# Four-layer recurrent network on one core: angle passes inside the first attention, third gating inside the last attention's set-up, one bias on GpSimd and one decay on VectorE

## The chip, the cores and the metric

The kernel runs on one core of one Trainium2 chip, as one program with one launch. The metric is device time in microseconds. The engines are named as the profile names them: PE (TensorE matmuls; PEld its weight loads), DVE (VectorE), ACT (ScalarE), POOL (GpSimd), SP (SyncE, which issues most DMAs).

## The reference

Four layers, each of two parts. `x` has 4096 tokens (8 x 512, or the same tokens in other groupings) of 128 features; everything is float32. Each layer is

```python
xn = layernorm(x)
s = attention(xn)          # L0 sliding window, L1 recurrence, L2 local + latent, L3 see below
g = silu(ffn(xn))          # L0 low-rank quantised, L1 experts, L2 see below, L3 soft slots
x = x + s * g              # "gating"
```

What the change touches is in the third feed-forward and the last attention:

```python
# L2 ffn
real = x @ cos(theta + theta_noise);  imag = x @ sin(phi + phi_noise)
return sqrt(real * real + imag * imag)

# L3 attention: 16 heads of 64 complex features
ang = t[:, None, None] * om                       # t: position, om: frequencies
qr, kr = q * (cos(ang) + i sin(ang)), k * (cos(ang) + i sin(ang))
E = exp(clip(-mu * |t - t'|, -30, 0))             # per head: "decay"
V = sigma2 / (2 mu) * (1 - E * E) + eta2 + gamma2 # per head: "variance"
maha = max(|q|^2 + E * E * |k|^2 - 2 E * Re(qr . conj(kr)), 0) / V
logits = coef * log1p(maha / nu) - 32 * log(V)
logits = where(t >= t', logits, -inf)             # causal
out = softmax(logits) @ v @ Wo
```

`coef * log1p(maha / nu)` is computed as `coef * log(maha * V + nu * V)` with `coef * log V` taken into a second table, so a head has three tables over the causal half of the positions (128 x 1280): `E`, `V` (nu times the variance) and `G` (log of the variance times a factor of the head, and -1e30 where the key is later than the query: "bias").

## The kernel before

The activations lie transposed in SBUF (features on the partitions, tokens along the row): `x`, `xn` and `s`, 128 x 4096 each, are there for the whole program. `network` runs the parts one after the other: `layer_norm`, attention, feed-forward with its gating (`gated_add`), four times. A planner places the instructions: each goes to its engine by program order and by when its inputs, its tile memory and the engine are expected to be ready, so that an instruction without a mark can move ahead of earlier ones into idle time. An instruction issued through `net.in_order(engine)` is marked: marked instructions of one engine keep their order among themselves. Tile memory is a stack of pools; a tile in memory that an earlier pool held waits until that pool's last reader is done.

*First attention* (`l0_attention`, L203). 64 units `u` of half of the heads for 128 queries. In unit `u` PE turns the weights of `u` (`turned`), ACT copies them (`pt`), PE makes the scores of `u + 3` (`sc`), DVE scales and masks them (`e`) and takes the maximum (`mx`), POOL subtracts it, ACT takes the exponential of `u + 2`, and PE weighs the values (`weigh`, `av`). In every second unit DVE divides the sums (`norm`: `rec`, then `o`) and PE turns them (`tpo`). All of it is marked.

*Angles and sines* (`Prepared.angles`, L1968, and `sines`, L1985). For each of four groups of features DVE multiplies the positions by the frequencies (`ang`, 128 x 512), reduces the angle to one turn (`turn`, L1270: six passes over `ang` and `turns`) and takes the absolute value (`cos`). ACT then makes the cosines, sines and negated sines (128 x 2048 each), and SP stores the three in DRAM (`trig`), from where each head of the last attention loads its own (`ct`, `sn`). Before, all of this lies between the third attention and the last one: `angles` in front of `l2_ffn`, `sines` behind it.

*Third feed-forward* (`l2_ffn`, L1281). 16 matmuls of 128 x 512, squares on ACT, a sum on DVE (`g`), square roots and silu on ACT (marked), and the gating: DVE multiplies (`pr`), POOL adds to `x`.

*Last attention* (`l3_attention`, L1309). The set-up makes the distances `dt` and the causal mask `later` (0 or -1e30, 128 x 1280) on POOL and DVE, the tables of head 0 (`Tables`: `decay`, `exp`, `squares`, `variance`, `variance_nu`, `log`, `bias`), the products `wvo` of the value and output weights (`ps_vo`), and then the norm. The main loop runs over 64 pairs of batches (4 per head) in software-pipelined steps: `STEP` is an order written out by hand, in which `"1 rotate 0"` is part `rotate` of batch 0 of the pair one ahead of the step's, and `"T1 decay"` is part `decay` of the next head's tables, in each fourth step with remainder 1. All of it is marked, so every engine works through `STEP` in this order. The parts that the texts name: `rotate` (DVE, `r<-sn`, `r<-ct`, and a DMA `rs<-r` on SP that swaps halves), `turned` (POOL, `r<-r,rs`), `scores` (PE, `sc<-r`), `key_terms` (POOL, four `ek<-E,kn`), `halved`, `scaled`, `distances` (DVE), `log` (ACT), `logits` (DVE, `y<-y,coef,G`), `maxima` (DVE), `exps` (ACT), `turn`, `weigh`, `values` (PE), `normalise` (ACT), `add` (POOL, `s<-s,o`). ACT's table sets for logarithm and exponential are loaded twice a step.

In the profile, marked instructions all bear line L82 (the helper), so they are told apart by their tiles.

Of the kernel before, what the change touches and what calls it, by code (L numbers as in the profile page):

```python
# [16 lines left out]
P = 128  # L17
B = 8
S = 512
# [183 lines left out]
def l0_attention(net, xn, s_out):  # L203
# [6 lines left out]
    with ExitStack() as st:  # L210
# [152 lines left out]
        for u in range(N + 2):  # L363
# [17 lines left out]
            next(todo, None)  # L381

# [887 lines left out]
def turn(nc, pool, ang, shape, tag):  # L1270

    k = pool.tile(shape, F32, tag=tag, name=tag)
    nc.vector.tensor_scalar(k, ang, 1.0 / (2 * math.pi), ROUND, ALU.mult, ALU.add)
    nc.vector.tensor_scalar(k, k, ROUND, None, ALU.subtract)
    for part in TWO_PI_PARTS:
        nc.vector.scalar_tensor_tensor(ang, k, -part, ang, ALU.mult, ALU.add)
    pi = float.fromhex("0x1.921fb4p+1")
    nc.vector.tensor_scalar(ang, ang, pi, -pi, ALU.min, ALU.max)
# [30 lines left out]
def l3_attention(net, x, xn, s_out):  # L1309
# [9 lines left out]
    with ExitStack() as st:  # L1319
        p1 = st.enter_context(tc.tile_pool(name="a3_1", bufs=1))  # L1320
        pw = st.enter_context(tc.tile_pool(name="a3_w", bufs=2))
        p2 = st.enter_context(tc.tile_pool(name="a3_2", bufs=2))
        p3 = st.enter_context(tc.tile_pool(name="a3_3", bufs=3))
# [7 lines left out]
        later = p1.tile([P, PK], F32, tag="later", name="later")  # L1331
        nc.gpsimd.memset(later, 0.0)
        with tc.tile_pool(name="a3_d", bufs=1) as pd:
            di = pd.tile([P, PK], I32, tag="di", name="di")
            for i in range(NQ):
                cols = slice(off[i], off[i] + w[i])
                nc.gpsimd.iota(di[:, cols], pattern=[[-1, w[i]]], base=P * i, channel_multiplier=1)
                nc.gpsimd.affine_select(
                    out=later[:, cols], in_=later[:, cols], compare_op=ALU.is_ge, fill=NEG,
                    base=P * i, pattern=[[-1, w[i]]], channel_multiplier=1,  # L1340
                )
# [17 lines left out]
        class Tables:  # L1359
# [24 lines left out]
            def decay(self):  # L1384
                pool.tensor_scalar(self.E, dt, nmu[:, self.hs], -30.0, ALU.mult, ALU.max)
# [20 lines left out]
            def bias(self):  # L1406
                G = self.G
                dve.scalar_tensor_tensor(G, G, g_v[:, self.hs], later, ALU.mult, ALU.add)
# [5 lines left out]
        with tc.tile_pool(name="a3_v", bufs=2, space=PSUM) as p_v, tc.tile_pool(  # L1414
            name="a3_vw", bufs=2
        ) as p_vw:
            for g in range(4):
# [9 lines left out]
                nc.scalar.copy(wvo[:, 4 * g : 4 * g + 4, :], ps)  # L1427
            net.layer_norm(x, xn)

        p_s = st.enter_context(tc.tile_pool(name="a3_s", bufs=1, space=PSUM))  # L1430
# [9 lines left out]
        class Pair:  # L1440
# [188 lines left out]
            "0 scores 1", "-1 exps 0 3", "1 key_lengths 0", "-1 exps 0 0", "-1 turn 0 2",  # L1629
            "T1 decay", "0 halved 1", "-1 keep 0 2", "1 key_terms 0", "1 query_norms 0",  # L1630
            "-1 turn 0 0", "-1 exps 1 0", "-2 normalise 1", "1 query_lengths 0", "1 project 1 0",
            "1 turned 0", "0 scaled 1", "-1 exps 1 1", "-1 turn 0 1", "0 distances 1",
            "-1 keep 0 0", "1 project 1 1", "-2 add 0", "-1 keep 0 1", "1 rotate 1", "-1 weigh 0",
            "-1 inverse", "-1 turn 1 2", "0 log", "-1 turn 1 1", "0 logits", "T3 log",
            "1 scores 0", "T3 bias", "0 maxima 2", "-1 keep 1 2", "1 squares 1", "-1 keep 1 1",
            "0 values 0", "1 turned 1", "1 key_norms 1", "-1 normalise 0", "2 project 0 0",
            "0 keep_values 0", "1 halved 0", "1 key_lengths 1", "1 query_norms 1", "0 maxima 1",
            "-1 turn 1 0", "1 query_lengths 1", "T2 variance", "2 project 0 1", "0 exps 0 1",
            "0 values 1", "1 key_terms 1", "-1 keep 1 0", "T2 variance_nu", "-2 add 1", "T1 exp",
            "-1 weigh 1", "1 scaled 0", "2 squares 0", "0 maxima 3", "0 exps 1 2", "T1 squares",  # L1640
            "0 exps 1 3", "1 distances 0", "2 rotate 0", "2 key_norms 0", "0 keep_values 1",
# [498 lines left out]
```

## Time and profile before

| | us |
|---|---|
| median of the 3 runs | 2870.13 |
| lowest, highest | 2869.78, 2882.57 |
| the profiled execution | 2865.32 |
| its span, first to last instruction | 2863.6 |

Where the stages lie in the span (from the timeline, us): first norm and first attention to about 315, first feed-forward to 440, second norm to 466, the second layer to 890, third norm to 923, third attention to 1250, third gating to 1289, norm of the last layer (with the set-up of the last attention around it) to 1329, last attention's pairs to about 2700, last feed-forward to the end.

A line of a group has the engine, operation, tiles (output<-inputs), shape and count, then busy us and mean ns of one, then the idle time before it and who ended it. A line of the timeline has start, duration, engine, operation and tiles. In a busy table each engine's column is busy us with the number of instructions in brackets. A line of the waits has who waited for whom, us in total, times and the longest.

### The profile page before, as it was taken

How to read it: one execution, taken by the hardware profiler on the slowest of the kernel's cores; microseconds unless marked ns; L12 is line 12 of the kernel's file. 1: busy time of each engine (PE TensorE's matmuls, PEld its weight loads, DVE VectorE, ACT ScalarE, POOL GpSimd, SP SyncE). 2: the span in 40 equal slices, each digit the busy share in tenths (PEclk: the TensorE clock that was granted, in tenths of full speed). 3: DMA queues.
4: the chain of work that ended last, by engine and by line, in shares of the span. 5: the costliest groups of instructions: out<-in, count | busy, mean ns of one | idle time of the engine just before them, and what ended most of it. 6: DMA issues, size and time to landing. Idle time of an engine off the chain costs nothing. (4 is left out here: it accounts for less than half of the span.)

```text
span 2863.6 us, 48763 instructions
## 1 busy us (share of the span) xinstructions
PE 2575.9 (90%) x18636; PEld 1801.4 (63%) x18636; DVE 2195.4 (77%) x2907; ACT 1835.7 (64%) x3587; POOL 1556.8 (54%) x1262
## 2 busy tenths in 40 slices
PE   7999898688778889977999999999999999999887
PEld 5666666455335555535677777677777777777674
DVE  4777454566663666664999999999999999999565
ACT  2666342245331455452899888898888889888734
POOL 2444221532342333335677877877877787777323
PEclk7999797899898899877999999999999999999989
DMA  1000002112100000003222222222222222222000
GB/s 48 2 2 2 1 1 89 30 51 46 32 28 17 2 2 2 2 23 92 62 61 57 49 62 61 61 61 57 54 57 61 62 56 66 55 52 52 25 1 30
DMA packets 56310, 112.73 MB, mean 39 GB/s; under 512 B 10768, under 2 KB 28752, under 8 KB 55440
## 3 DMA queue, kind: packets, MB, share of 16 engines
q1 hardware_dynamic: 51584, 99.40, 13.2%
q0 software_dynamic: 4352, 8.92, 1.3%
q8 instruction: 148, 2.42, 0.4%
q10 hardware_dynamic: 144, 1.31, 0.1%
q14 instruction: 82, 0.67, 0.1%
HBM read 30.43 MB, written 12.06 MB: 15 GB/s over the span
## 5 line engine op out<-in xcount | busy, mean ns | idle before, releaser
L82 POOL TENSOR_TENSOR ek<-E,kn 128x512 f32<-128x512 f32 (+3 forms) x512 | 427.1, 867 | 63.2 <-ACT kn L82 62.1
L82 POOL TENSOR_TENSOR r<-r,rs 128x1024 f32<-128x1024 f32 x128 | 317.9, 2484 | 252.9 <-DMA rs<-r 213.1
L82 POOL TENSOR_TENSOR e<-e,mx 128x1024 f32<-128x1024 f32 x112 | 212.6, 1898 | 333.8 <-DVE mx L82 195.5
L82 ACT ACTIVATE y<-y,mx 128x256 f32<-128x256 f32 (+3 forms) x512 | 287.2, 562 | 101.2 <-DVE mx L82 101.1
L82 PE MATMUL sc<-r 128*128 128x512 f32 (+3 forms) x1024 | 307.9, 444 | 24.6 <-POOL r L82 18.8
L82 PEld LDWEIGHTS ps_av<-u,at 128*128 128x128 f32 x2560 | 302.3, 193 | 41.2 <-ACT at L82 31.3
L82 PE MATMUL ps_av<-u,at 128*128 128x128 f32 x2560 | 315.1, 279 | 6.5 <-ACT at L82 6.5
L82 PEld LDWEIGHTS sc<-r 128*128 128x128 f32 x1024 | 166.4, 192 | 176.5 <-issue 71.7
L82 DVE SCALAR_TENSOR_TENSOR y<-sc,qn,V 128x512 f32<-128x512 f32 (+3 forms) x512 | 246.0, 543 | 2.3
L82 ACT ACT_TABLE_LOAD x167 | 214.3, 1283 | 4.1 <-PE pa L82 1.2
L82 DVE TENSOR_REDUCE mx<-y 128x2 f32<-128x768 f32 (+3 forms) x256 | 207.7, 812 | 1.7
L82 DVE SCALAR_TENSOR_TENSOR sc<-sc,ek 128x1280 f32<-128x1280 f32 x128 | 191.3, 1495 | 12.5 <-PE sc L82 6.2
L82 PE MATMUL tp<-ident,y 128*128 128x128 f32 x1280 | 198.5, 278 | 1.2 <-ACT y L82 0.8
L82 DVE SCALAR_TENSOR_TENSOR y<-y,coef,G 128x2560 f32<-128x2560 f32 x64 | 195.7, 3058 | 4.6 <-ACT y L82 2.3
L82 ACT COPY at<-tp 128x512 f32<-128x512 f32 (+1 forms) x384 | 188.2, 512 | 7.8 <-PE tp L82 7.7
L82 DVE TENSOR_TENSOR sc<-sc,E 128x1280 f32<-128x1280 f32 x128 | 191.1, 1493 | 0.0
L82 PEld LDWEIGHTS tp<-ident,y 128*128 128x128 f32 x1280 | 154.3, 146 | 41.4 <-issue 18.3
L82 POOL TENSOR_TENSOR s<-s,o 128x512 f32<-128x512 f32 x120 | 162.6, 1356 | 31.1 <-ACT o L82 31.1
L82 PEld LDWEIGHTS ps_u<-wvo,xn 128*128 128x128 f32 x1024 | 128.3, 191 | 69.2 <-DVE qn L82 55.2
L82 DVE TENSOR_TENSOR r<-sn,ps_kq 128x1024 f32<-128x1024 f32 x128 | 154.9, 1210 | 7.6 <-ACT sq L82 4.1
L82 ACT ACTIVATE y<-y 128x2560 f32<-128x2560 f32 x64 | 149.7, 2339 | 15.6 <-DVE y L82 8.1
L82 PE MATMUL tp<-ident,e 128*128 128x128 f32 x896 | 135.0, 294 | 23.6 <-ACT rt L82 14.4
(396 smaller groups left out, 5779.4 us busy)
## 6 DMA issues: line engine op xcount, KB each, us to landing
rs<-r SPq DMA_DIRECT2D x256, 256.0 KB
yrows<-yy SPq DMA_DIRECT2D x36, 128.0 KB
ct<-trig SPq DMA_DIRECT2D x16, 256.0 KB
m_w<-m_w SPq DMA_DIRECT2D x1, 2560.0 KB
x<-x SPq DMA_DIRECT2D x8, 256.0 KB
xrows<-row SPq DMA_DIRECT2D x8, 256.0 KB
sn<-trig SPq DMA_DIRECT2D x32, 64.0 KB
sn<-trig SPq DMA_DIRECT2D x16, 128.0 KB
```

Of the source, the lines that this page charges most:

```text
L82: ins = op(*args, **kwargs)
```

## The change

- The angle passes become a generator (`turning`, and `angles` with a `yield` after each pass). `network` opens it before the first attention (load of the frequencies and the iota of the positions), and `l0_attention` issues one pass, marked on DVE, at the end of each of the first eight units and of every odd unit after that.
- `angles` now uses the pool of the first layer (`prep_0`), which stays open over the second norm; `sines` (three ACT operations and three DMAs on SP) follows that norm.
- `l2_ffn` is called inside `l3_attention`, after the tables of head 0 and `wvo` and before the norm; the pools `a3_2` and `a3_3` open after that.
- `later` is gone. `bias` multiplies on POOL and sets the causal corner of each query tile with four `affine_select` of 128 x 128 on POOL; `decay` moves from POOL to DVE.
- `STEP` has a new order; `decay` and `exp` of the next head's tables move from remainder 1 to 0.

```diff
--- before.py
+++ after.py
@@ -200,7 +200,7 @@
             )
 
 
-def l0_attention(net, xn, s_out):
+def l0_attention(net, xn, s_out, extra):
 
 
     nc, tc = net.nc, net.tc
@@ -379,6 +379,10 @@
             if u >= U and u % U == 1:
                 finish(u // U - 1)
             next(todo, None)
+            if u % 2 or u < 8:
+                next(extra, None)
+        for _ in extra:
+            pass
 
 
 def l0_ffn(net, x, xn, s):
@@ -1269,13 +1273,23 @@
 
 def turn(nc, pool, ang, shape, tag):
 
+    for _ in turning(nc.vector, pool, ang, shape, tag):
+        pass
+
+
+def turning(dve, pool, ang, shape, tag):
+
     k = pool.tile(shape, F32, tag=tag, name=tag)
-    nc.vector.tensor_scalar(k, ang, 1.0 / (2 * math.pi), ROUND, ALU.mult, ALU.add)
-    nc.vector.tensor_scalar(k, k, ROUND, None, ALU.subtract)
+    dve.tensor_scalar(k, ang, 1.0 / (2 * math.pi), ROUND, ALU.mult, ALU.add)
+    yield
+    dve.tensor_scalar(k, k, ROUND, None, ALU.subtract)
+    yield
     for part in TWO_PI_PARTS:
-        nc.vector.scalar_tensor_tensor(ang, k, -part, ang, ALU.mult, ALU.add)
+        dve.scalar_tensor_tensor(ang, k, -part, ang, ALU.mult, ALU.add)
+        yield
     pi = float.fromhex("0x1.921fb4p+1")
-    nc.vector.tensor_scalar(ang, ang, pi, -pi, ALU.min, ALU.max)
+    dve.tensor_scalar(ang, ang, pi, -pi, ALU.min, ALU.max)
+    yield
 
 
 def l2_ffn(net, x, xn, s):
@@ -1319,8 +1333,6 @@
     with ExitStack() as st:
         p1 = st.enter_context(tc.tile_pool(name="a3_1", bufs=1))
         pw = st.enter_context(tc.tile_pool(name="a3_w", bufs=2))
-        p2 = st.enter_context(tc.tile_pool(name="a3_2", bufs=2))
-        p3 = st.enter_context(tc.tile_pool(name="a3_3", bufs=3))
 
         sp, nmu, v_e2, v_0, coef, k_0, q_0, g_v = net.prep.scalars
         nu = sp[:, 3, :]
@@ -1328,17 +1340,11 @@
         wvo = p1.tile([P, H, P], F32, tag="wvo", name="wvo")
 
         dt = p1.tile([P, PK], F32, tag="dt", name="dt")
-        later = p1.tile([P, PK], F32, tag="later", name="later")
-        nc.gpsimd.memset(later, 0.0)
         with tc.tile_pool(name="a3_d", bufs=1) as pd:
             di = pd.tile([P, PK], I32, tag="di", name="di")
             for i in range(NQ):
                 cols = slice(off[i], off[i] + w[i])
                 nc.gpsimd.iota(di[:, cols], pattern=[[-1, w[i]]], base=P * i, channel_multiplier=1)
-                nc.gpsimd.affine_select(
-                    out=later[:, cols], in_=later[:, cols], compare_op=ALU.is_ge, fill=NEG,
-                    base=P * i, pattern=[[-1, w[i]]], channel_multiplier=1,
-                )
             nc.vector.tensor_copy(dt, di)
         nc.vector.scalar_tensor_tensor(dt, dt, -1.0, dt, ALU.mult, ALU.max)
 
@@ -1382,7 +1388,7 @@
                 )
 
             def decay(self):
-                pool.tensor_scalar(self.E, dt, nmu[:, self.hs], -30.0, ALU.mult, ALU.max)
+                dve.tensor_scalar(self.E, dt, nmu[:, self.hs], -30.0, ALU.mult, ALU.max)
 
             def exp(self):
                 table_set("exp_and_others")
@@ -1404,8 +1410,15 @@
                 act.activation(self.G, self.G, AF.Ln)
 
             def bias(self):
+
                 G = self.G
-                dve.scalar_tensor_tensor(G, G, g_v[:, self.hs], later, ALU.mult, ALU.add)
+                pool.tensor_scalar(G, G, g_v[:, self.hs], 1.0, ALU.mult, ALU.mult)
+                for i in range(NQ):
+                    last = G[:, off[i] + P * i : off[i] + P * i + P]
+                    pool.affine_select(
+                        out=last, in_=last, compare_op=ALU.is_ge, fill=NEG,
+                        base=0, pattern=[[-1, P]], channel_multiplier=1,
+                    )
 
         tables = {}
         T = tables[0] = Tables(0)
@@ -1425,8 +1438,11 @@
                         ps[:, i, :], lhsT=wv[:, i, :], rhs=wo[:, i, :], start=True, stop=True
                     )
                 nc.scalar.copy(wvo[:, 4 * g : 4 * g + 4, :], ps)
+            l2_ffn(net, x, xn, s_out)
             net.layer_norm(x, xn)
 
+        p2 = st.enter_context(tc.tile_pool(name="a3_2", bufs=2))
+        p3 = st.enter_context(tc.tile_pool(name="a3_3", bufs=3))
         p_s = st.enter_context(tc.tile_pool(name="a3_s", bufs=1, space=PSUM))
         p_kq = st.enter_context(tc.tile_pool(name="a3_kq", bufs=1, space=PSUM))
         p_j = st.enter_context(tc.tile_pool(name="a3_j", bufs=2, space=PSUM))
@@ -1626,20 +1642,20 @@
 
 
         STEP = (
-            "0 scores 1", "-1 exps 0 3", "1 key_lengths 0", "-1 exps 0 0", "-1 turn 0 2",
-            "T1 decay", "0 halved 1", "-1 keep 0 2", "1 key_terms 0", "1 query_norms 0",
-            "-1 turn 0 0", "-1 exps 1 0", "-2 normalise 1", "1 query_lengths 0", "1 project 1 0",
-            "1 turned 0", "0 scaled 1", "-1 exps 1 1", "-1 turn 0 1", "0 distances 1",
-            "-1 keep 0 0", "1 project 1 1", "-2 add 0", "-1 keep 0 1", "1 rotate 1", "-1 weigh 0",
-            "-1 inverse", "-1 turn 1 2", "0 log", "-1 turn 1 1", "0 logits", "T3 log",
-            "1 scores 0", "T3 bias", "0 maxima 2", "-1 keep 1 2", "1 squares 1", "-1 keep 1 1",
-            "0 values 0", "1 turned 1", "1 key_norms 1", "-1 normalise 0", "2 project 0 0",
-            "0 keep_values 0", "1 halved 0", "1 key_lengths 1", "1 query_norms 1", "0 maxima 1",
-            "-1 turn 1 0", "1 query_lengths 1", "T2 variance", "2 project 0 1", "0 exps 0 1",
-            "0 values 1", "1 key_terms 1", "-1 keep 1 0", "T2 variance_nu", "-2 add 1", "T1 exp",
-            "-1 weigh 1", "1 scaled 0", "2 squares 0", "0 maxima 3", "0 exps 1 2", "T1 squares",
-            "0 exps 1 3", "1 distances 0", "2 rotate 0", "2 key_norms 0", "0 keep_values 1",
-            "0 exps 0 2", "0 maxima 0",
+            "1 project 0 1", "0 key_terms 1", "-1 maxima 3", "-2 weigh 1", "-1 values 1",
+            "-1 exps 0 1", "1 squares 0", "-1 exps 1 1", "-1 exps 1 2", "1 key_norms 0",
+            "-1 keep_values 1", "-1 exps 0 3", "0 distances 0", "0 scores 1", "-1 exps 1 3",
+            "-1 turn 0 2", "1 key_lengths 0", "-1 exps 0 2", "-1 keep 0 2", "T1 squares",
+            "T0 decay", "-1 turn 0 0", "T2 variance", "1 rotate 0", "-1 maxima 0", "-1 exps 0 0",
+            "1 query_norms 0", "0 halved 1", "-1 keep 0 0", "0 scaled 1", "1 key_terms 0",
+            "-1 exps 1 0", "1 project 1 0", "-2 normalise 1", "1 query_lengths 0", "1 turned 0",
+            "-1 turn 0 1", "-1 keep 0 1", "1 project 1 1", "0 distances 1", "-1 weigh 0",
+            "1 rotate 1", "0 log", "-1 turn 1 2", "-1 turn 1 1", "-1 keep 1 2", "1 squares 1",
+            "T3 log", "1 scores 0", "-1 inverse", "-1 keep 1 1", "-1 normalise 0", "0 logits",
+            "-2 add 1", "0 maxima 1", "1 key_norms 1", "-1 turn 1 0", "1 key_lengths 1", "T3 bias",
+            "1 turned 1", "1 halved 0", "2 project 0 0", "T2 variance_nu", "-1 keep 1 0",
+            "0 maxima 2", "-1 add 0", "0 values 0", "T0 exp", "0 keep_values 0", "1 query_norms 1",
+            "1 scaled 0", "1 query_lengths 1",
         )
         for t in range(-2, N + 3):
             if t + 2 < N:
@@ -1975,12 +1991,17 @@
         ti = pt.tile([P, S], I32, tag="ti", name="ti")
         nc.gpsimd.iota(ti, pattern=[[1, S]], base=0, channel_multiplier=0)
         tt = pt.tile([P, S], F32, tag="tt", name="tt")
-        net.in_order(nc.vector).tensor_copy(tt, ti)
+        yield
+        dve = net.in_order(nc.vector)
+        dve.tensor_copy(tt, ti)
+        yield
         for g in range(4):
             a = self.ang3[:, g, :]
-            nc.vector.tensor_scalar(a, tt, om[:, g : g + 1], None, ALU.mult)
-            turn(nc, pt, a, [P, S], "turns3")
-            nc.vector.scalar_tensor_tensor(self.cos[:, g, :], a, -1.0, a, ALU.mult, ALU.max)
+            dve.tensor_scalar(a, tt, om[:, g : g + 1], None, ALU.mult)
+            yield
+            yield from turning(dve, pt, a, [P, S], "turns3")
+            dve.scalar_tensor_tensor(self.cos[:, g, :], a, -1.0, a, ALU.mult, ALU.max)
+            yield
 
     def sines(self):
 
@@ -2046,19 +2067,20 @@
         prep = net.prep = Prepared(net, ctx)
         with tc.tile_pool(name="prep_0", bufs=1) as p0:
             net.layer_norm(x, xn)
-            l0_attention(net, xn, s)
+            angles = prep.angles(p0)
+            next(angles)
+            l0_attention(net, xn, s, angles)
             prep.l0_decode(p0)
             l0_ffn(net, x, xn, s)
-        net.layer_norm(x, xn)
+            net.layer_norm(x, xn)
+            prep.sines()
         l1_layer(net, x, xn, s)
         net.layer_norm(x, xn)
         with tc.tile_pool(name="prep_t", bufs=1) as pt:
             prep.l2_weights(pt)
             l2_attention(net, xn, s)
-            prep.angles(pt)
             prep.l3_scalars()
-            l2_ffn(net, x, xn, s)
-            prep.sines()
+
         l3_attention(net, x, xn, s)
         l3_ffn(net, x, xn, s, out)
```

## Prediction

> **What bounds the kernel now.** I read the page first: no engine is the bound of the whole, and DVE goes from about half busy to 9 tenths in slices 24 to 37.
>
> ```profile
> PE 2575.9 (90%) x18636; PEld 1801.4 (63%) x18636; DVE 2195.4 (77%) x2907; ACT 1835.7 (64%) x3587; POOL 1556.8 (54%) x1262
> DVE  4777454566663666664999999999999999999565
> ```
>
> Then the busy time by stage (columns: stretch, its length, busy us of PE, PEld, DVE, ACT, POOL, granted clock, DMA share, GB/s), for the four stages that the change touches:
>
> ```profile
> 60.00:120.00 60.00, 57.30 (x684) 36.89 (x682) 38.90 (x44) 36.86 (x58) 26.15 (x15) 0.90 0.01 2
> ...
> 1250.00:1292.00 42.00, 26.05 (x50) 11.50 (x51) 32.25 (x46) 29.41 (x39) 12.87 (x8) 0.70 0.16 66
> 1292.00:1340.00 48.00, 39.10 (x177) 32.37 (x177) 15.78 (x23) 10.56 (x15) 23.77 (x18) 0.69 0.31 91
> ...
> 1440.00:2600.00 1160.00, 1129.43 (x6637) 828.99 (x6636) 1147.62 (x1342) 1035.46 (x2181) 913.21 (x715) 1.00 0.23 58
> ```
>
> The first attention (60:120) is PE's, the last attention's loop (1440:2600) is DVE's: 12 us of 1160 idle. Between them, 1250:1340 (third gating, set-up and norm of the last attention) is bound by no engine: a chain. Third, the loop's groups by shape (busy us, mean ns):
>
> ```profile
> L82 DVE SCALAR_TENSOR_TENSOR y<-y,coef,G 128x2560 f32<-128x2560 f32 x56 | 172.6, 3082 | 2.0
> L82 DVE SCALAR_TENSOR_TENSOR G<-G,g_v,later 128x1280 f32<-128x1280 f32 x13 | 20.1, 1545 | 0.0
> L82 POOL TENSOR_SCALAR E<-dt,nmu 128x1280 f32<-128x1280 f32 x14 | 64.3, 4592 | 1.3
> L82 POOL TENSOR_SCALAR V<-G,sp 128x1280 f32<-128x1280 f32 x14 | 18.7, 1339 | 0.0
> ```
>
> Fourth, POOL's and DVE's timelines around one `y<-y,coef,G` that is longer than the rest (start, duration):
>
> ```profile
> 1538.63 4.59 POOL L82 TENSOR_SCALAR E<-dt,nmu 128x1280 f32<-128x1280 f32 x1
> 1543.29 3.33 POOL L82 TENSOR_TENSOR ek<-E,kn 128x512 f32<-128x512 f32 x4
> 1546.58 2.39 POOL L82 TENSOR_TENSOR r<-r,rs 128x1024 f32<-128x1024 f32 x1
> 1548.91 1.29 POOL L82 TENSOR_TENSOR s<-s,o 128x512 f32<-128x512 f32 x1
> ...
> 1548.88 4.00 DVE L82 SCALAR_TENSOR_TENSOR y<-y,coef,G 128x2560 f32<-128x2560 f32 x1
> ...
> 1193.37 1.50 DVE L82 TENSOR_SCALAR xp<-xp 128x64 f32<-128x64 f32 x1
> ```
>
> To see: the decay (`E<-dt`) makes POOL late by 4.59 us; its `s` add then falls on DVE's logits, which take 4.00 instead of 2.885: the two exclude each other. The last line is a one-input DVE operation that takes 0.20 us elsewhere and 1.50 us against a POOL subtraction.
>
> From start to start of the 64 logits (1361.26 to 2683.13) are 63 steps, 1321.9 us. An undisturbed step is 20.40 us, and 63 of them are 1285.2. The other 36.7 us lie in two steps of each four: 21.74 where the bias `G<-G` runs on DVE (+1.34), about 21.5 where POOL carries the decay.
>
> **Part 1, the last attention's loop (15 heads; head 0 is in the set-up).** Removed from DVE: 15 biases at 1.34 us of pace: -20.1. Removed from POOL: the decay, 4.59 us a head, and with it the late steps: 36.7 - 20.1 = -16.6. POOL takes the bias instead: one multiply like `V<-G,sp` (same operation, 1.34) and four 128x128 selects at the 0.29 of the `later` select, 2.5 us. Its table work falls from 9.65 (4.59 + 2.32 + 1.40 + 1.34) to 7.6 a head, and is spread over more steps.
> Added to DVE: the decay. Nearest row: `ang<-tt,a_om` 128x512, 0.474 us with one scalar from memory; DVE's copy `dt<-di` of 128x1280 takes 0.82. So 0.87, 0.80 of pace: +12.0. It also needs what POOL holds. It stands behind `distances 0`, where POOL is about in its four `ek` (1.27, 1.00, 0.73, 0.46). Bounds: 0 us, and the rest of such a run, 3.3. The `xp` row waited for one instruction; at 1548.88 POOL's next instruction went in ahead. I take 0.6, half of a long `ek`: +9.0. Behind the waiting decay are rotate 0, maxima 0 and halved 1, with ACT's exps waiting for the maxima.
> The written order is new throughout. Per step, start to start, PE needs about 19.6 us (from the back-to-back starts of 1441 to 1461) and ACT 18.3 with both table loads; so it can keep 20.40, but PE has 0.8 to spare. Where ACT takes `T3 log` (1.25) between squares 1 and keep 1 1, PE's values are late by more than that: +0.2 a head, +3.0 (ends 0 and 0.5 a head).
> Sum: -20.1 - 16.6 + 12.0 + 9.0 + 3.0 = **-12.7 us**.
>
> Two rules of the Trainium skill stand against this part. "GPSIMD Engine Reference", Engine selection, sends elementwise work to VectorE but calls GpSimd's one-input operations roughly line-rate. The V row agrees (1.34); the decay row (4.59) doesn't. By the rule the decay costs POOL 1.3 us, its removal wins little, the -16.6 goes, and part 1 is +3.9; by the row, -12.7. The row decides. "SBUF — State Buffer", in its section on the two sides, says that whichever of the two engines starts first keeps the shared ports for the whole instruction; then a waiting decay pays for one POOL instruction (1.27 at most of an `ek`), not for a run. The 1548.88 row leaves the run open.
>
> **Part 2, third gating inside the set-up.** Now the set-up's work for head 0 lies in the norm behind the gating. After the last `x` add this norm takes 39.9 us, where the second norm takes 25.5:
>
> ```profile
> 437.66 2.87 POOL L162 TENSOR_TENSOR x<-x,pr 128x512 f32<-128x512 f32 x2 [4.17 <-DVE pr L161]
> 465.36 0.69 DVE L141 TENSOR_TENSOR xn<-xn,ps 128x512 f32<-128x512 f32 x1 [0.21 <-PE ps L101]
> ...
> 1276.07 12.87 POOL L162 TENSOR_TENSOR x<-x,pr 128x512 f32<-128x512 f32 x8 [28.48 <-DVE pr L161]
> 1328.10 0.69 DVE L141 TENSOR_TENSOR xn<-xn,ps 128x512 f32<-128x512 f32 x1 [1.02 <-PE ps L101]
> ```
>
> In between lie decay 4.6, squares and two scalings 5.1, `later` 3 us on POOL in front of or between the `rstd` powers; the three sines (2.0 + 1.9 + 1.9 and a table load) on ACT in front of the squares; 6.3 us of `ps_vo` matmuls on PE. With these in front: 25.5 - 39.9 = -14.4. They come into the gating's 17 us of matmuls, where POOL idles 28 us. POOL's 6.5 to 7.6 us and DVE's decay are covered there. PE isn't idle: `ps_vo` adds 0 to 6.3 us. ACT's sum there is 9.6 of squares, 2.3 of copies, 2.5 for exp and log, 2.6 for loads: 17.0, as long as the matmuls. I take +4. The loop's first logarithm comes behind the gating's square root and silu now and needs its table again: 1.28 on an ACT that idles 7.25 us in front of it, so 0. The set-up's eight weight loads and table 0's six on SP come before a norm that needs none of them. Sum **-10.4 us** (ends -14 and 0). The angle passes (about 18 us on DVE) leave this stage too, but it isn't DVE's: its `g` adds wait for ACT. I count 0.
>
> **Part 3, the angles in the first attention.** 33 passes: one copy 0.42 and four times 0.47 + 0.42 + 0.42 + 3 x 0.69 + 0.42 + 0.69: 18.4 us of DVE. Cover: in 60:300 DVE waits 50.1 us for PE's scores. Against it: PE waits for DVE's `o` already:
>
> ```profile
> DVE e L82 <- PE sc L82: 50.1, 36, 4.2
> PE tpo L82 <- DVE o L82: 3.5, 14, 0.2
> ```
>
> A pass sits behind a unit's maximum, ahead of the next norm (`rec`, `o`), for which PE's `tpo` waits, and against POOL's subtraction (1.90 us), for which ACT's exp waits. About half of the norms have no slack (14 of 29), and each is pushed by 0.3 to 0.6: 14 x 0.45 = 6; some of it comes back. I take **+5 us** (ends 0 and 18.4, or 25 with POOL's turns). The iota (0.56 on POOL) and the small load move to the start, in front of nothing.
>
> **Part 4, sines behind the second norm.** 5.8 us and a load of 1.28 on ACT, ordered only against marked ACT work, so they can fall into gaps of the first feed-forward or into the norm: 0 to 7, I take 1. Their three 1 MB stores go into SP's queue there, and their memory, with the norm now stacked on it, must be free before the next layer's loads: `m_w` was issued at 440.5 and used at 537 (slack), the router weights are used at 466, at once: 0 to 4, I take 1. **+2 us.**
>
> **Sum**: -12.7 - 10.4 + 5 + 2 = -16.1 us. The profiled execution took 2865.3 (span 2863.6), so 2849; the median of the three runs is 2870.1, 4.8 above it: **2854 us**. A difference under 0.5% (14 us) is about what a measurement here can't tell from none.
>
> **Rivals.**
> - *The decay is held by POOL (slower).* If POOL's queued instructions keep going in ahead, a decay that meets the run of `ek` waits 3.3 us: 15 x (3.3 - 0.6) = +40, 2894. For: 1548.88. Against: the rule, `xp`. From a mean wait of 1.7 us the whole gain is gone, from 2.6 it is slower by over 0.5%. PE with its 0.8 us to spare would show alike: 0.8 us of new waits in 50 steps is 40 us.
> - *The moved work lands on the path.* Passes 18, gating +6 beyond my 4, loads 4: 16.1 of gain less 13 + 6 + 2 more: 2875, within 0.5%. For: PE busy 57 of 60 us in the first attention.
> - *All is covered.* No decay wait, no late log (-12), passes and sines free (-7), `ps_vo` free (-4): 2831.
> - *It doesn't do what it says*: the marks order only marked work, so sines or set-up may stay where they collide; then -10.4 shrinks to about 0: 2864.
>
> **Numbers.** Forecast 0.55 (own range 2836 to 2868), work on the path or not moved 0.19, held decay or PE 0.18, all covered 0.08. Faster: 0.42 of the forecast's 0.55 and the 0.08, 0.50. Slower: the 0.18 and 0.03 of the second: 0.21. Same: 0.29. The range leaves out half of the held case and a little at the bottom: 2832 to 2888.
>
> **What would show it.** Right: logits 2.89 throughout, steps of 20.4 with one of about 21.8 in four; E on DVE 0.9 to 1.5; last `x` add to last `xn` about 26 us; PE's wait for `o` up by some us in the first attention. Wrong: E on DVE over 2.5; undisturbed steps over 20.6 (the order, PE); a norm still near 40; a first attention longer by over 12.

## The result and the profile after

The changed kernel takes 2903.15 us (median of 7 runs, 2893.29 to 2911.06), the kernel before, run beside it, 2868.86 (2863.51 to 2882.57): a ratio of 1.0109, interval 1.0081 to 1.0137. It is slower by 1.1%, where 2854 was forecast. The profiled execution took 2911.06 against 2865.32, a span of 2909.3 against 2863.6: 45.7 us to explain. The medians lie 34.3 apart: the profiled execution of the kernel after is the slowest of its seven, and that of the kernel before is 3.5 under its median.

First the page: the engines' sums, and the rows of DVE and of the granted TensorE clock. The kernel after:

```profile
PE 2618.5 (90%) x18636; PEld 1828.8 (63%) x18636; DVE 2185.2 (75%) x2907; ACT 1845.1 (63%) x3588; POOL 1513.3 (52%) x1321
DVE  4566635446665466663799999999999999999665
PEclk8687768789989889897899999999999999999979
```

and the clock row of the kernel before, which the prediction left out:

```profile
PEclk7999797899898899877999999999999999999989
```

PE has the same 18636 matmuls and is busy 42.6 us longer. In slices 1 to 4 its clock row has 6877 where it was 9997: the first attention. Then the busy table over exactly that attention, from its first projection to its last sum (stretch, length, busy us of PE, PEld, DVE, ACT, POOL, granted clock, DMA share, GB/s), before:

```profile
45.75:321.20 275.45, 257.15 (x3264) 168.29 (x3264) 189.29 (x217) 167.91 (x265) 123.41 (x67) 0.94 0.01 2
```

and after:

```profile
42.51:387.38 344.87, 320.74 (x3264) 206.27 (x3264) 208.19 (x250) 170.54 (x265) 126.28 (x67) 0.74 0.01 1
60.00:120.00 60.00, 55.65 (x502) 35.75 (x500) 35.14 (x42) 25.18 (x40) 19.88 (x10) 0.66 0.00 1
```

The stage is 69.4 us longer. DVE has the 33 passes more (217 to 250 instructions, busy 18.9 us longer). PE's idle time (length less busy) grows from 18.3 to 24.1, by 5.8 us; its busy time grows by 63.6 us for the same 3264 matmuls. So the passes made PE wait hardly longer, but made it run slower: the clock fell from 0.94 to 0.74. "Clock lost" below is the length times what the clock lacks of 1, added up from the trace's clock record: 16.5 us before, 88.8 after, a difference of 72.3.

How one drop begins, from the timeline of after (start, duration, idle time ahead and who ended it):

```profile
196.04 0.74 DVE L82 TENSOR_SCALAR s<-ps_o,a_b 128x512 f32<-128x512 f32 x1
196.70 0.80 DVE L82 TENSOR_SCALAR kb<-ps_k,hm,kbias 128x512 f32<-128x512 f32 x1
197.42 1.32 DVE L82 SCALAR_TENSOR_TENSOR cos<-ang 128x512 f32<-128x512 f32 x1
...
198.66 0.24 DVE L82 RECIPROCAL rec<-av 128x16 f32<-128x16 f32 x1
198.94 0.29 DVE L82 TENSOR_TENSOR o<-av,rec 128x128 f32<-128x128 f32 x1
...
199.38 0.44 PE L82 MATMUL tpo<-ident,o 128*128 128x128 f32 x1 [0.87 <-ACT pt L82]
...
199.75 1.88 PE L82 MATMUL av<-vw,pt 128*64 128x9 f32 x32
...
201.56 2.08 PE L82 MATMUL ps_q<-xn,a_w 128*128 128x512 f32 x2
```

The pass `cos` (1.32 against a POOL subtraction, 0.69 in the kernel before) stands ahead of `rec` and `o`, and `tpo` starts behind a PE gap of 0.87. The profile puts this gap down to ACT's copy `pt`, which ended 0.04 us after `o`; at the same place of before, `tpo` starts at 203.06 without a gap while these copies still run (202.83 to 203.89), so the wait is for `o`. At once `av` takes 1.88 (1.12 at 193.74) and `ps_q` 2.08 (`ps_o`, of the same shape, 1.12 at 194.79): about half speed. The busy table around it:

```profile
189.10:196.00 6.90, 6.54 (x88) 4.31 (x89) 5.39 (x5) 4.12 (x6) 3.07 (x2) 1.00 0.01 2
196.00:199.40 3.40, 2.05 (x17) 0.79 (x15) 3.37 (x7) 1.74 (x3) 1.90 (x1) 1.00 0.01 2
199.40:202.80 3.40, 3.40 (x35) 2.64 (x36) 2.18 (x2) 1.31 (x2) 0.94 (x1) 0.50 0.00 0
```

One stretch of 3.4 us with PE busy 2.05, and the next is at 0.50. How one persists, another stretch of after:

```profile
141.40:165.30 23.90, 23.90 (x166) 14.19 (x165) 12.44 (x16) 9.52 (x15) 7.60 (x4) 0.50 0.01 1
```

PE is busy all of 23.9 us and stays at half. "TensorE: Matmul & The Clock Gate" of the Trainium skill, Part 1 (The HAM clock gate), gives a window of about 3.4 us: half speed after at least one idle window, full speed after one busy one. The window agrees: the lengths in the record (6.8, 13.7, 20.5, 23.9) are multiples of 3.41. The conditions do not: no window ahead of a drop was idle (of the nine drops after 60 us, seven follow gaps of at most 0.9 us, the others of 2.0 and 2.6), and seven busy windows in a row did not bring the clock back. By this rule, if a window is called idle or busy by PE's busy time, this attention would have lost next to no clock; by the record it lost 88.8 us. The measurement decides. The page's section on a second failure mode, micro-idling between groups of matmuls, comes nearer to what is seen.

The waits in 60:300, after:

```profile
DVE e L82 <- PE sc L82: 74.8, 35, 5.2
PE tpo L82 <- DVE o L82: 8.1, 9, 2.6
```

PE's wait for `o` grew from 3.5 to 8.1, and the waits of PE that the view lists in this stretch sum to 13.1 where they were 9.4. That is the size of the prediction's +5 us, and it is all that PE's waits show of a cost of 69.

Last, the loop's groups by shape (1440:2600, busy us, mean ns), and its busy table:

```profile
L82 DVE SCALAR_TENSOR_TENSOR y<-y,coef,G 128x2560 f32<-128x2560 f32 x56 | 161.6, 2885 | 2.2
L82 POOL TENSOR_SCALAR G<-G,g_v 128x1280 f32<-128x1280 f32 x14 | 23.6, 1687 | 46.3 <-ACT G L82 46.3
L82 DVE TENSOR_SCALAR E<-dt,nmu 128x1280 f32<-128x1280 f32 x14 | 19.2, 1375 | 0.0
L82 POOL TENSOR_SCALAR V<-G,sp 128x1280 f32<-128x1280 f32 x14 | 18.7, 1334 | 0.0
L82 POOL TENSOR_SCALAR_AFFINE_SELECT G<-G 128x128 f32<-128x128 f32 x56 | 14.6, 292 | 1.0
```

```profile
1440.00:2600.00 1160.00, 1140.12 (x6726) 839.67 (x6726) 1151.55 (x1360) 1055.34 (x2212) 878.84 (x776) 1.00 0.24 60
```

All logits take 2.885 us now (3.082 before), and the steps are 20.40 with one of 21.56 in four. From the first to the last logits it is 1301.8 us, 20.0 less than before.

The account of the 45.7 us, from stage to stage of the two traces: first attention +69.4; router's matmuls, behind the second norm, +8.8; last attention's loop -20.0; third gating, set-up and norm up to the first logits -3.5 (110.9 to 107.4); first norm -3.2; all else -5.8.

### The profile page after: what moved, and what is told of

Its sections match the earlier page's. It is cut to its first block, busy times and chain, and to the rows that moved or that the text cites. A ratio compares the mean times of both kernels' runs of the same rounds, so it can differ in the third digit from the quotient of the medians.

```text
span 2909.3 us, 49020 instructions
## 1 busy us (share of the span) xinstructions
PE 2618.5 (90%) x18636; PEld 1828.8 (63%) x18636; DVE 2185.2 (75%) x2907; ACT 1845.1 (63%) x3588; POOL 1513.3 (52%) x1321
## 5 line engine op out<-in xcount | busy, mean ns | idle before, releaser
L82 POOL TENSOR_TENSOR ek<-E,kn 128x512 f32<-128x512 f32 (+3 forms) x512 | 435.7, 885 | 48.5 <-ACT kn L82 48.4
L82 POOL TENSOR_TENSOR r<-r,rs 128x1024 f32<-128x1024 f32 x128 | 302.3, 2362 | 237.2 <-DMA rs<-r 215.7
L82 ACT COPY at<-tp 128x512 f32<-128x512 f32 (+1 forms) x384 | 198.4, 517 | 43.2 <-PE tp L82 41.8
L82 DVE TENSOR_REDUCE mx<-y 128x2 f32<-128x512 f32 (+3 forms) x256 | 207.6, 812 | 2.2
L82 PE MATMUL tp<-ident,y 128*128 128x128 f32 x1280 | 183.3, 274 | 9.3 <-ACT at L82 7.5
L82 DVE SCALAR_TENSOR_TENSOR y<-y,coef,G 128x2560 f32<-128x2560 f32 x64 | 184.6, 2885 | 4.9 <-ACT y L82 2.3
L82 PE MATMUL tp<-ident,e 128*128 128x128 f32 x896 | 155.4, 325 | 22.6 <-ACT rt L82 14.4
L82 DVE SCALAR_TENSOR_TENSOR e<-sc,maskFalse 128x1024 f32<-128x1024 f32 (+1 forms) x96 | 90.2, 954 | 108.0 <-PE sc L82 108.0
L82 PEld LDWEIGHTS tp<-ident,e 128*128 128x128 f32 x896 | 125.5, 168 | 64.5 <-issue 34.6
L82 ACT COPY pt<-tp 128x512 f32<-128x512 f32 x224 | 121.8, 584 | 66.5 <-PE tp L82 66.0
```

Of the source, the lines that this page charges most:

```text
L82: ins = op(*args, **kwargs)
```

## The experiments

The theory was the clock: a pass ahead of the norm opens a gap on PE, the clock falls to half and stays there until a batch's dense projections come. The rival was the queue: every pass and its turn with POOL lengthen the chain DVE, POOL, ACT by 2 us (33 x 2 = 66), and a slow PE only follows. Each ratio below is to executions of before made beside that run (their medians are 2856.9 to 2867.1), so times of different runs are compared by their ratios. The table gathers what the profiles show of the first attention, one profile of each kernel.

| kernel | attention, us | clock lost, us | length less clock lost |
|---|---|---|---|
| before | 275.4 | 16.5 | 258.9 |
| after | 344.9 | 88.8 | 256.1 |
| p_after | 276.1 | 16.9 | 259.3 |
| p_even | 299.4 | 42.1 | 257.3 |
| p_fill | 304.4 | 32.7 | 271.6 |
| fill_only | 280.6 | 12.3 | 268.3 |
| b_extra | 331.0 | 69.9 | 261.1 |
| b_late | 317.4 | 52.9 | 264.5 |
| b_early | 293.4 | 32.3 | 261.1 |
| b_late6 | 364.3 | 100.1 | 264.2 |
| b_early6 | 308.5 | 39.9 | 268.6 |

**Is it the passes' place?** `p_after` issues them behind the attention, `b_extra` adds 33 such passes to the kernel before.

```diff
-            l0_attention(net, xn, s, angles)
+            l0_attention(net, xn, s, iter(()))
+            for _ in angles:
+                pass
```

> The changed kernel with its 33 angle passes in one run on VectorE behind the first attention instead of one a unit inside it; all else as changed. Clock theory (the passes hold up the norm, TensorE gets gaps, its granted clock falls to half and stays there until the next batch's projections): half-clock time inside the first attention falls from 178 us to about 33, the attention from 345 to about 275, and 18 us of passes lie in the first feed-forward, partly beside its 30 us of other work: the kernel comes to 2830 to 2850. Queue theory (each pass lengthens the VectorE-GpSimd-ScalarE chain by 2 us, the clock only follows): the same stage time, so this run does not tell the two apart; it says whether the passes' place costs the whole 69 us. If the attention stays over 300, the cause is another part of the change (memory layout, an earlier load).

2839.54 us, a ratio to before of 0.9934 (0.9910 to 0.9957); the attention is back at 276.1. So the whole 69 us came with the passes' place. The executions without a kept trace agree: over the seven of each kernel, the span times the granted clock is 2638 to 2649 us in after and 2634 to 2645 in `p_after`, while the clock lost is 255 and 196 us in the mean.

> The kernel before with 33 further passes of the same shapes in the first attention, one at the end of each odd unit and of the first eight, their results never used; nothing else is changed. Both theories: the attention goes from 275 to about 345 and the kernel from 2869 to about 2938, with half-clock time near 178 us. If it costs under 30 us, the passes alone are not the cause and something else of the change in that stage is.

2911.46 us, 1.0192 (1.0162 to 1.0221); +55.6 us on the attention, of which 53.4 clock. Less than the 70 expected, but most of the cost comes with the passes alone; the changed memory layout and loads are in `p_after` too and cost its attention nothing.

**Queue or clock?** Three kernels keep all 33 passes inside. `p_even` issues them, from the ninth unit on, in front of the scores' `e` instead of the norm:

```diff
-            if u % 2 or u < 8:
+            if u % 2 == 0 or u < 8:
```

> The changed kernel with the same 33 passes, still one a unit inside the first attention, at the end of even units (and of the first eight) instead of odd ones: ahead of the next scores, which VectorE waits for anyway, instead of ahead of the next norm. Clock theory: TensorE's wait for o disappears, the half-clock time falls to 30 to 70 us and the attention to 280 to 300; the kernel comes to 2835 to 2855. Queue theory: the same number of passes in the same chain cost the same, attention about 345, kernel about 2903.

2846.25 us, 0.9960 (0.9950 to 0.9969); attention 299.4. The same DVE work costs 24 us here and 69 there, and both differences are clock (25.6 and 72.3). Up to 115 us, which takes in the first eight units, with a pass each in both kernels, both lose 26 us of clock; behind that `p_even` loses 16 and after 63. `p_fill` gives PE more to do:

```diff
+            pe.matmul(
+                tp[:, 2:4, :], lhsT=net.ident, rhs=w[:, 0:2, :], start=True, stop=True
+            )
             pe.transpose(tp[:, 0, :], o.rearrange("p h d -> p (h d)"), net.ident)
```

> The changed kernel with the passes where the change put them, and one further matmul (identity by 128x256 of weights, its result never read) on TensorE ahead of each of the 32 transposes tpo: it fills the gap in which TensorE waits for o. Clock theory: the gaps are gone or shorter and a dense matmul lies in each, so the clock stays at full speed for most of the attention; although TensorE has 32 x 0.56 = 18 us more to do, the attention falls from 345 to 285 to 310. Queue theory: more work on the busiest engine can only lengthen it: 345 to 363.

2848.64 us, 0.9965 (0.9947 to 0.9983). The busy table over its attention:

```profile
43.56:347.93 304.37, 288.35 (x3328) 186.73 (x3328) 209.17 (x250) 169.16 (x265) 126.50 (x67) 0.89 0.01 2
```

Against after it has 64 matmul records more, the same passes, and PE is busy 32 us less: the added work made the busiest engine faster, 0.89 of the clock instead of 0.74. The queue theory cannot give that. What the added matmuls cost without the passes:

> The version with the passes behind the first attention, with the further matmul ahead of each tpo but no passes in the attention: what the 32 matmuls cost alone. TensorE is busy 57.3 us of 60 there, so up to 32 x 0.56 = 18 us on the attention, less what clock they bring back out of the 16.5 us that are lost there without them: 276 to 294. With the passes the same matmuls gave 304 instead of 345. If they cost nearly nothing here, those 41 us were gained by filling alone; if 18, the gain in clock was about 59.

2846.52 us, 0.9927 (0.9913 to 0.9942); attention 280.6. They cost some 9 us of work (last column of the table; 18 were expected at most) and win back 4.6 of clock. With passes, they won 56 of clock (88.8 to 32.7) for 15 of work.

**What ends a drop?** Holds, four multiplies of a scratch tile each, in the kernel before, at the same number and in two places:

```diff
             next(todo, None)
+            if u in HELD:
+                for _ in range(4):
+                    dve.tensor_scalar(junk, junk, 1.0, None, ALU.mult)
```

> The kernel before with three holds in the first attention: four VectorE multiplies of a 128x512 scratch tile (4 x 0.42 = 1.7 us, result unused) ahead of the norm that follows units 13, 29 and 45, the sixth unit of a batch, when the projections of the next batch are three to four units away. Clock theory: each hold opens a gap on TensorE, the clock falls to half and stays there until those projections, 20 to 30 us: 3 x (1 + 10 to 15) = 33 to 48 us on the attention. Queue theory: a hold costs at most its own length, 3 x 1.7 = 5 us.

> The same three holds of 1.7 us after units 9, 25 and 41, the second unit of a batch, directly ahead of the projections of q and v for the next batch. Clock theory: the clock is either not lost or is back within 3 to 7 us: 3 x (1 + 2 to 4) = 9 to 15 us on the attention, a third of the other place. Queue theory: 5 us, no difference between the two places.

Attention +42.0 and +18.0 in the profiles, but medians of 2887.29 (1.0101, 1.0077 to 1.0126) and 2875.72 (1.0083, 1.0055 to 1.0111): the intervals overlap, and three holds did not settle it. So six:

> The kernel before with six holds of 1.7 us of VectorE work (results unused) in the first attention, ahead of the norm behind the sixth unit of batches 2 to 7 (units 13, 21, 29, 37, 45, 53). The three holds at this place cost 42 us of the attention in the profile, of which 36 were clock. Clock theory: each hold costs the rest of its batch at half clock, so six cost about twice as much, 70 to 90 us, and the kernel is 55 us or more above the kernel before. Queue theory: 6 x 1.7 = 10 us.

> The same six holds behind the second unit of batches 2 to 7 (units 9, 17, 25, 33, 41, 49), ahead of the projections of q and v. The three at this place cost 18 us in the profile, 8.5 of which may be a drop at the attention's start that lies ahead of the first hold. Clock theory: six cost 20 to 30 us on the attention, a third of the late place, and the times of the two kernels lie 40 us or more apart. Queue theory: 10 us, the two agree.

2950.97 us (1.0275, 1.0241 to 1.0309) and 2905.72 (1.0134, 1.0100 to 1.0168): 45 us apart. The busy tables of the two attentions, late first:

```profile
43.56:407.90 364.34, 330.65 (x3264) 212.42 (x3264) 208.03 (x241) 170.54 (x265) 123.44 (x67) 0.73 0.01 1
```

```profile
46.40:354.88 308.48, 278.48 (x3264) 181.39 (x3264) 201.97 (x241) 169.16 (x265) 123.17 (x67) 0.87 0.01 2
```

The same six holds cost 89 us in one place and 33 in the other. They were not equally long: one multiply of each meets a POOL subtraction, so a late hold took 3.3 us of DVE and an early one 2.3, where 1.7 was meant. PE's idle time (length less busy) was 33.7 and 30.0, though, so 4 us of the 56 between the two are waiting and 60 are clock (100.1 and 39.9). Ahead of the next batch's 128x512 matmuls most drops are short (one of the early six lasted 20.5 us); far from them they last.

**Gap, or work fed?** The kept traces hold a measure that sorts the clock better than gaps do. For each window of 3.41 us, add up the columns of PE's matmuls in it, each weighed by its tile's share of the 128x128 array (`av`, 128\*64, by a half; `sc`, 32\*64, by an eighth). A bound of 1489 columns, taken from the first attention of before and after (2 of 179 windows on the wrong side), gives the clock of the next window in 1275 of the 1282 windows of the other fifteen traces. The best bounds on PE's busy time and on its longest gap, chosen on all 1461, are wrong in 275 and 271; to say that the clock stays as it is errs in 183. Two windows of `p_after` in a row:

```profile
136.06:139.48 3.42, 3.20 (x46) 2.01 (x47) 2.70 (x6) 2.58 (x5) 1.50 (x1) 1.00 0.00 0
139.48:142.89 3.41, 3.41 (x14) 1.94 (x16) 1.01 (x1) 1.65 (x3) 1.90 (x1) 0.50 0.00 0
```

They feed 1398 and 1973 columns. In the first PE is busy 3.20 us with no gap over 0.14, and the clock still drops behind it; behind the second it is back. In after, the window ahead of the drop at 199.4 feeds 1387. The six half-speed windows from 141.4 to 161.8 feed 886 to 1461 with PE busy throughout, and the seventh, with the next batch's projections, 1558; then the clock is back. At full clock this attention feeds 1844 columns a window in the mean, so a fifth of a window lost to a wait is enough for a drop; at half clock it feeds 1216, under the bound, and stays down until dense work comes. This was read from traces taken for other ends, and no run was made to test it. It holds for this stage only: over the rest of the program the same bound is wrong in 761 of 12791 windows, 616 of them in the second layer.

**The last attention's loop.** The decay back on POOL, in the changed order (on top of `p_after`):

```diff
-                dve.tensor_scalar(self.E, dt, nmu[:, self.hs], -30.0, ALU.mult, ALU.max)
+                pool.tensor_scalar(self.E, dt, nmu[:, self.hs], -30.0, ALU.mult, ALU.max)
```

> The changed kernel with the passes behind the first attention and, in the last attention's loop, the decay back on GpSimd (bias stays there too, the changed order stays). By the prediction's terms: VectorE gets 12.0 + about 7 us of decay and its wait back, GpSimd gets 4.59 us a head more and is late again, 16.6 us or more over the loop, since it now carries both: loop 1302 - 19 + 17 to 1302 - 19 + 50, so 1300 to 1335, with logits over 3.5 us again in some steps. Rival (GpSimd's late steps were not what cost the 16.6 us, the old order was): loop about 1285, faster than the changed one.

2882.08 us, 1.0090 (1.0059 to 1.0121). The loop is 1337.8 us, 35.7 more than `p_after` and just over the expected end; the logits' mean is up again, by shape:

```profile
L82 DVE SCALAR_TENSOR_TENSOR y<-y,coef,G 128x2560 f32<-128x2560 f32 x54 | 172.2, 3189 | 2.1
L82 POOL TENSOR_SCALAR E<-dt,nmu 128x1280 f32<-128x1280 f32 x14 | 64.3, 4592 | 1.3
```

So the decay on POOL makes logits late and costs time in the new order too. The old order with the decay on DVE was not run.

**Gating and angles.** `back34` is the changed kernel with angles and sines where they were; `gate_out` is `p_after` with the third gating ahead of the set-up again.

```diff
-            l2_ffn(net, x, xn, s_out)
             net.layer_norm(x, xn)
```

> The changed kernel with the angle passes and the sines where the kernel before has them (behind the third attention); the third gating stays inside the last attention's set-up, and the last attention's loop is the changed one. Attention back at 275 us, the first router matmuls at once behind the second norm (0 instead of 7 us) and 12.1 us long instead of 13.8, the loop at 1302. Open is the stretch from the third attention to the first logits (before 110.9 us, changed 107.4): the passes (18 us on VectorE) and sines (7 us on ScalarE) lie in it again. If they hide beside the gating as before, it stays at 107 to 111 and the kernel is 20 to 25 us faster than the kernel before; if they delay the norm there, up to 120, and it is 8 to 15 us faster.

> The changed kernel with the passes behind the first attention, and the third gating again ahead of the last attention's set-up, as in the kernel before; no angle work lies in that stretch. From the third attention's last copy to the first logits: 110.9 us in the kernel before (angles there, gating outside), 110.1 with angles there and gating inside, 104.1 to 107.4 with angles elsewhere and gating inside. Prediction's term: the gating's place brings 10.4 less, the angles nothing, so this run is at 111. Rival: the gain is that of the angles and sines gone from the stretch, so this run is at 104 to 107 too, and the place of the gating is worth nothing.

`back34`: 2832.54 us, 0.9918 (0.9900 to 0.9935). `gate_out`: 2839.70 beside another set of runs of before (2866.88), 0.9900 (0.9881 to 0.9918): the two lowest ratios of all, both faster than either kernel. Their intervals overlap, and `back34`'s overlaps that of `p_after`, so these are not told apart. From the third attention's last copy to the first logits:

| us | gating outside | gating inside |
|---|---|---|
| angles and sines there | 110.9 (before) | 110.1 (back34) |
| angles and sines elsewhere | 100.3 (gate_out) | 107.4 (after), 104.1 (p_after) |

My expectation for `gate_out` (111) was wrong; its rival (104 to 107) had the direction. With the angles gone, the gating's new place costs 4 to 7 us: the other profiles agree, 98.3 and 99.6 outside (`free_sines`, `sines_ffn`) and 104.1 to 107.4 inside (`p_even`, `p_fill`, `fill_only`, `decay_pool`). With the gating inside, the angles' and sines' leaving is worth 3 to 6. The column of the gating outside is not clean: `gate_out` has the changed set-up too. Between the norm's `rstd` powers, POOL no longer has `later` (2.9 us) and the decay (4.6 us), and has the bias (2.4 us) instead. So its 10.6 under before are the angles, the sines and the set-up together; no run has the new set-up with the angles there and the gating outside.

**A home for the passes.** Putting them into the third attention:

> The version with the gating inside the set-up and the angles behind the third attention, with the 33 angle passes put ahead of the third attention instead, where they fall into its first units between its own VectorE work; the sines stay behind it. The stretch from the third attention to the first logits should fall from 110 to about 105. If the passes hide in the third attention, the kernel gains 5 us on 2833; if they open gaps on TensorE there and the clock falls, it loses 5 to 20 us.

2856.46 us, 0.9965 (0.9951 to 0.9978). The stretch to the first logits falls to 106.7, but that attention takes 15 us more than in `back34`; the clock lost there is 57.3 us against 41.2, 16 more. The same loss again. Behind the first attention (`gate_out`) the passes cost its feed-forward 7.7 us instead. Two runs tried to lower that and the router's delay:

> The version with the passes behind the first attention and the third gating ahead of the set-up, with the sines (5.8 us and two table loads of 1.28 on ScalarE) put behind the passes into the first feed-forward instead of behind the second norm. Their stores then end some 80 us before the second norm does. If these stores hold the memory that the router weights wait for: the router's first matmul comes at once behind the norm, 5 us are gained there, and the feed-forward pays 0 to 8 us: 2832 to 2840 where the version without it has 2840. Rival (the load waits for something else, such as its place in the queue): still 5 us behind the norm.

> As the run before it, with the angle passes free to be ordered among the first feed-forward's VectorE work instead of in one fixed run. The 33 passes cost 8 to 10 us of that feed-forward in a fixed run; if it is their fixed order that costs, the stretch from the attention's end to the second norm's start falls by 4 to 8 us; if it is VectorE's 18 us as such, it stays.

2848.14 us (0.9935, 0.9922 to 0.9948) and 2853.81 (0.9959, 0.9945 to 0.9973), both no better than `gate_out`: the sines cost the feed-forward 6 us there, and free order wins nothing, which fits a cost of DVE's time itself. The router's wait, first in after, then in `sines_ffn` (waits of PE):

```profile
PE ps_lg L82 <- DMA m_r<-m_r: 7.8, 1, 7.8
```

```profile
PE ps_lg L82 <- DMA m_r<-m_r: 3.3, 1, 3.3
```

`gate_out`, with the stores behind the norm, waits 5.8, and the seven kernels that have them there wait 5.0 to 7.8. `free_sines`, like `sines_ffn`, waits 3.3. So the stores explain some 2 to 4 us of the wait; in `sines_ffn` the load goes out at 478.7, as the norm ends, which fits memory held by the norm that is now stacked on `prep_0`. That was not tried alone.

## Why the prediction was wrong

- **Part 3, the step that failed**: "each is pushed by 0.3 to 0.6: 14 x 0.45 = 6 ... I take +5 us (ends 0 and 18.4, or 25 with POOL's turns)". The wait was sized well (`tpo` for `o`: +4.6; PE idle: +5.8), and the attention cost 69.4. The missing term is the granted clock: the sum priced a wait by its length, and the runs show that such waits lower the clock for many times that length, 72.3 us of clock for 5.8 of idle time. The clock stood in the windows that the prediction shows (0.90 in 60:120) and was not used; no end of the range held it. The trace of before already had the effect: 3.4 us at half speed at 236.0, behind a window with PE busy 0.84.
- **The rival "The moved work lands on the path"** priced the passes at 18 us, their own length: wrong as well. Length less clock lost is 258.9 before and 256.1 after; as DVE time the passes cost nothing that one profile of each can show (the eight kernels with neither passes nor other additions in this attention have 255.5 to 260.2).
- **Part 1** forecast -12.7, measured -20.0. The 36.7 us over undisturbed steps are gone (-20.1 and -16.6; no logits is late, and with POOL carrying the decay they are late again), and 16.6 have come where 24.0 were taken (12.0 + 9.0 + 3.0). Oversized were the decay's wait and the late logarithm: E took 0.887 undisturbed and 1.375 in the loop, 0.49 of wait for 0.6, and the one long step in four is 1.16 over the others where 0.80 + 0.6 + 0.2 = 1.6 was taken. A decay held by a run of POOL instructions did not appear: no E in the loop took over 1.41 us, so "SBUF — State Buffer", its section on the two sides (one instruction's wait), was the better guide than the row at 1548.88.
- **Part 2** forecast -10.4, measured -3.5, and for the wrong reason. The last `x` to last `xn` did fall, from 39.9 to 29.9:

```profile
1353.85 12.90 POOL L162 TENSOR_TENSOR x<-x,pr 128x512 f32<-128x512 f32 x8 [16.04 <-DVE pr L161]
...
1395.98 0.69 DVE L141 TENSOR_TENSOR xn<-xn,ps 128x512 f32<-128x512 f32 x1 [1.02 <-PE ps L101]
```

  But `gate_out` has 30.8 there with the gating outside, and `back34`, with both inside, gives its 30.7 back in a gating 9 us longer. Two terms were mis-sized: "25.5 - 39.9 = -14.4" brought 9.9, and "+4" for `ps_vo` in the gating became its end of 6.3 (the gating went from 38.6 to 44.9, its matmuls from 17.0 to 23.3). "The angle passes leave this stage too ... I count 0" failed as well: their leaving, with the sines, is worth 3 to 6 us with the gating inside.
- **Part 4** forecast +2, measured about +9: the load of the router's weights was bounded at 4 behind the norm and came 7.1 behind it, and the 64 matmuls took 1.7 more (13.8). The second of these is also in `back34` and in `b_late6`, the kernel before with holds, which have no such wait, so it is not the change's.

Sum of the misses in the profiles: +64 (part 3), +7 (part 4), +7 (part 2), -7 (part 1), and -9 in stages that the forecast left at zero. Between the medians the miss is 49.

## What to carry to other kernels

Where PE runs near its limit on many small matmuls, a delay on another engine is not priced by its length: read the granted clock of the stage, and compare length less clock lost between two kernels before looking for a longer chain. A busy PE is no safety if its matmuls use small tiles. Put work that may delay PE where dense matmuls follow soon, or where PE is not the bound; if it must stay, fill the gap on PE with a matmul nobody needs. In a table of two edits run all four corners, alike in everything else, before a gain is given to one of them.

## What the runs showed of the hardware

- PE at half clock can be busy without a gap and stay there (23.9 us); an extra 128x256 matmul ahead of each of 32 transposes took 56 us off the clock lost.
- In the first attention the columns fed in a window of 3.41 us, weighed by tile size, tell the next window's clock in 1275 of 1282 windows not used for the bound; PE's busy time does not.
- Half-clock stretches come in multiples of 3.41 us. The same attention code lost 16.9 us in `p_after` and 26.6 in `decay_pool`, where only the last attention differs; the stage took 276.1 and 282.1, and the longest drop differs at its start (13.7 us and 34.1 us at 54). So one profile of such a stage is good to no better than 6 us.
- POOL needs 4.59 us for the decay (a multiply and a clamp, 128x1280) where it needs 1.33 for the variance of the same size; DVE does the decay in 0.887.
